# Turning the experts' inner units in row halves of the array

## The chip, the cores and the metric

The kernel runs on one core of one Trainium2 chip. The metric is the device time of one execution, in microseconds (us), of that core. A time is the median of several runs. The engines have short names: PE (TensorE, matmuls), PEld (its weight loads), DVE (VectorE), ACT (ScalarE), POOL (GpSimd), SP (the engine that issues most DMAs). PSUM, into which PE writes, is used here as eight banks of 128 partitions by 512 fp32 numbers.

## The reference

Two layers over x of shape (8, 512, 256), all fp32. The first adds to x a causal attention with 16 heads and a layer of 32 experts; the second adds a small two-layer network and a masked feed-forward layer. The change concerns the experts, which are, cut to what matters:

```python
probs = softmax(x @ gate_w.T + gate_b, axis=experts' tokens)
vals, idx = top_k(probs, 8)                 # eight tokens for each expert and batch
merged = sum over the eight of x[idx] * vals      # one row for each (batch, expert)
h = gelu(merged @ w1[e][:256] + w1[e][256])       # 256 -> 1024, last row is the first bias
o = h @ w2[e][:1024] + w2[e][1024]                # 1024 -> 256
out[b, idx] += o * vals
```

With 8 batches each expert has eight rows; the kernel pads them to 32 columns.

## The kernel before

Everything is laid out by a planner (class `Plan`). The code creates operations with `op(engine, cost, function, dependencies, priority, ...)`; `emit` then places them one by one on the engines, by the priorities and by the times that it reckons from the costs, and that fixes each engine's order of instructions. `acq` names what an operation takes: "b" is one PSUM bank, "w" is a pair of banks (there are four pairs), "eh" and "ehT" are single SBUF buffers. `rel` gives it back, at an entry such as `(tn, "w", 0, 2)` when the second of two readers is done.

Each PE operation has a mode. "R" stands for matmuls in row halves: two matmuls, one on partitions 0 to 63 and one on 64 to 127, each 64 rows deep, that write two different banks. "F" stands for the whole array, "E" and "C" for column slices. A change of mode adds `SWITCH` (96) to the cost in the planner, and a change to "F" a further `SECOND`; `choose` also prefers an operation in the mode of the one before it by `SAME`, half a unit of priority. These are the planner's numbers, not measured times.

The attention stage takes the largest part of the time. For each batch and each group of four heads (`produce`, 32 such groups) the queries, keys and values are projected, two tiles of 128 tokens at a time. `cross` (L337) runs a projection in two parts, all in row halves; between them the halves change places, and a VectorE memset of one small tile ("seen", L362) makes the second part wait until the first has been written. The projected tile tm is normalised and turned (L840, L330); `attend` computes scores, a softmax and the turned probabilities pr. `turn_halves` (L318) is the helper with which x, tm, gtm and pr are turned: for each block of 128 columns it issues two transposes, one for each half of the partitions, into the two banks of a pair.

The experts are spread through that stage, in eight groups of four (`expert`, L1177). A group runs like this:

- `hidden`: two halves of 512 inner units. Four experts at once write 32 partitions each of one bank (L1195); `h_out` copies the bank to `s.h`, the buffer eh (L1202).
- `turn`: four transposes of 128x128 for each half, in mode "F", into one bank (L1216). Partition and expert thereby become columns: the 128 columns of a block are four experts of 32.
- `bias`: one VectorE addition for each half, 512 numbers wide, of the turned first bias `eb1T` into the buffer ehT (L1227).
- `gelu`: ScalarE, in place, once both halves are added (L1222).
- `down`: the second weights, 32 columns at a time, out of ehT (L1255), and an addition into the output rows (L1262).

Weights are loaded by SP into a ring of five buffers. After the attention stage the outputs are joined (`combine`), and the second layer runs batch by batch.

Of the kernel before, what the change touches and what calls it, by code (L numbers as in the profile page):

```python
# [15 lines left out]
P = 128  # L16
# [3 lines left out]
H, D = 16, 64  # L20
# [9 lines left out]
EPG = 4  # L30
# [20 lines left out]
class Plan:  # L51
# [14 lines left out]
    def op(self, eng, cost, fn, deps, prio, acq=(), rel=(), mode="F", lat=0):  # L66
        o = Op()
        o.eng, o.cost, o.fn, o.prio, o.acq, o.rel, o.mode = eng, cost, fn, prio, acq, rel, mode
        o.deps = list(deps)
        o.end = lat  # L70
        self.ops.append(o)
        return o
# [148 lines left out]
def tile_two_layer_block(  # L221
# [26 lines left out]
    nc = tc.nc  # L248
# [12 lines left out]
    ident = const.tile([P, P], F32, tag="ident", name="ident")  # L261
# [27 lines left out]
    eb1T = const.tile([P, FH // P, E], F32, tag="eb1T", name="eb1T")  # L289
# [7 lines left out]
    with tc.tile_pool(name="pb", bufs=2) as pb, tc.tile_pool(name="pb1", bufs=1) as pb1:  # L297
# [8 lines left out]
        op = plan.op  # L306
# [3 lines left out]
        def w_tile(k=0):  # L310

            return plan.tile("w", k)

        def b_tile():

            return plan.tile("b")

        def turn_halves(dst, src, one=None, back=False):  # L318

            n = src.shape[1] // P
            for k in range(n):
                b = n - 1 - k if back else k
                for h in range(2):
                    rows = slice(h * D, (h + 1) * D)
                    out = dst[h][:, k * D : (k + 1) * D]
                    blk = src[rows, b * P : (b + 1) * P]
                    if one is None:
                        nc.tensor.transpose(out, blk, ident[rows, rows])  # L330
                    else:
                        nc.tensor.matmul(out, blk, one[rows, rows], start=True, stop=True)
# [81 lines left out]
        for q in range(NPR):  # L414
            consts.append(op("ACT", 675, lambda q=q: bias_rows(q), consts[1:2], -7.0 + 0.1 * q,
                             rel=["pr1"] if q == NPR - 1 else []))
# [72 lines left out]
        for k, f in enumerate(log1p_steps(lambda: oz, lambda: oy, lambda: oy2, lambda: om_sb)):  # L489
# [4 lines left out]
                   rel=["pr0"])]  # L494
# [155 lines left out]
        def turn_eb():  # L650
# [9 lines left out]
        v_eb = op("DVE", 334, lambda: nc.vector.tensor_copy(  # L660
            eb1T, early.pe[:, : FH // P * E].rearrange("p (k e) -> p k e", e=E)), [tb], 20.1,
            rel=[(tb, "b", 0)])
# [514 lines left out]
        def expert(g, when, ahead):  # L1177


            s = Grp()  # L1180
            s.pt = {}
            s.po = {}
            held = None
            out_ops = []
            for half in range(2):
                ld = load_stage(4 * g + half, when[half] - ahead)

                def hidden(half=half):
                    m = 4 * g + half
                    if half == 0:  # L1190
                        s.h = pb.tile([P, FH], F32, tag="eh", name=f"eh_{g}", bufs=1)
                    s.ph = b_tile()
                    for dc in range(NC):
                        for q in range(EPG):
                            nc.tensor.matmul(  # L1195
                                s.ph[32 * q : 32 * (q + 1), :], mT[:, dc, g * EPG + q, :],
                                ew[m, q][:, dc * 512 : (dc + 1) * 512],
                                start=(dc == 0), stop=(dc == NC - 1),
                            )

                def h_out(half=half):
                    nc.vector.tensor_copy(s.h[:, half * 512 : (half + 1) * 512], s.ph)  # L1202

                hd = op("PE", 1716, hidden, ld + merged, when[half], acq=["b"] + ["eh"] * (half == 0),
                        rel=["ew"] * EPG, mode="E")
                ho = op("DVE", 598, h_out, [hd], when[half] + 0.1, rel=[(hd, "b", 0)])

                def turn(half=half):
                    if half == 0:
                        s.hT = pb.tile(  # L1210
                            [P, FH // P, EPG, 32], F32, tag="ehT", name=f"ehT_{g}", bufs=1
                        )
                    s.pt[half] = b_tile()
                    for c in range(4):
                        k = half * 4 + c
                        nc.tensor.transpose(  # L1216
                            s.pt[half][:, c * P : (c + 1) * P], s.h[:, k * P : (k + 1) * P], ident
                        )

                def gelu(half=half):  # L1220
                    hT = s.hT[:, half * 4 : (half + 1) * 4]
                    nc.scalar.activation(hT, hT, AF.Gelu)  # L1222

                def bias(half=half):

                    c = slice(half * 4, (half + 1) * 4)
                    nc.vector.tensor_add(  # L1227
                        s.hT[:, c],
                        s.pt[half].rearrange("p (c q r) -> p c q r", c=4, q=EPG),
                        eb1T[:, c, g * EPG : (g + 1) * EPG].unsqueeze(3).to_broadcast(  # L1230
                            [P, 4, EPG, 32]
                        ),
                    )

                merged_used.append(hd)
                out_ops.append((ho, turn, bias, gelu))
            acts = []
            for half, (ho, turn, bias, gelu) in enumerate(out_ops):
                tn = op("PE", 436, turn, [out_ops[0][0], out_ops[1][0]], when[2] + 0.01 * half,
                        acq=["b"] + ["ehT"] * (half == 0), rel=["eh"] * (half == 1))  # L1240
                acts.append(op("DVE", 598, bias, [tn, v_eb], when[2] + 0.05 + 0.01 * half, rel=[(tn, "b", 0)]))
            gl = []
            for half, (ho, turn, bias, gelu) in enumerate(out_ops):
                gl.append(op("ACT", 586 + 1283 * (1 - half), gelu, acts, when[2] + 0.1 + 0.01 * half))
            prev = []
            for half in range(2):
                ld = load_stage(4 * g + 2 + half, when[3 + half] - ahead)

                def down(half=half):
                    m = 4 * g + 2 + half  # L1250
                    s.po[half] = b_tile()
                    for c in range(4):
                        for q in range(EPG):
                            k = half * 4 + c
                            nc.tensor.matmul(  # L1255
                                s.po[half][32 * q : 32 * (q + 1), :C], s.hT[:, k, q, :],
                                ew[m, q][:, c * C : (c + 1) * C],
                                start=(c == 0), stop=(c == 3),
                            )

                def o_out(half=half):
                    nc.vector.tensor_add(ebias[g], ebias[g], s.po[half][:, :C])  # L1262

                dn = op("PE", 1716, down, ld + gl, when[3 + half], acq=["b"],
                        rel=["ew"] * EPG + (["ehT", "eb"] if half else []), mode="E")
                prev = [op("DVE", 334, o_out, [dn] + prev,
                           when[3 + half] + 0.1, rel=[(dn, "b", 0)])]

            def o_send():
                for q in range(EPG):  # L1270
                    for hb in range(2):
                        nc.sync.dma_start(
                            o_all[g * EPG + q : P : E, hb, :],
                            ebias[g][32 * q + hb * BPG : 32 * q + (hb + 1) * BPG, :],
                        )

            experts_out.append(op("DMA", 500, o_send, prev, when[4] + 0.2, lat=2000))
# [14 lines left out]
        for g in range(NG):  # L1292
            h0, h1, d0, d1 = ((NHG + 2) * NU + step * (4 * g + k) + 0.7 for k in range(4))
            expert(g, [h0, h1, h1 + 3.0, d0, d1], step)
# [115 lines left out]
        for k in range(NFC // 2):  # L1410
# [9 lines left out]
            def out1(pt, k=k):  # L1420
# [6 lines left out]
                              merged_used, rel=["ew"] if k % 2 else []))  # L1427
# [389 lines left out]
```

## Time and profile before

| | |
|---|---|
| median of 3 runs | 1448.41 us (1447.43 to 1449.52) |
| the profiled execution | 1447.03 us, of which its span 1445.3 us |
| granted TensorE clock in it | 0.986 |
| first L1216 matmul, last | 287.6 us, 1016.5 us |
| first gelu of an expert group (L1222) | 294.4 us |
| first down product (L1255) | 315.9 us |

The span runs from the first to the last instruction; what lies around it is 1.7 us. Rows of the profile name the engine, the source line, the operation, and output<-inputs by the program's names. All PSUM banks are called w there, without a number. Many helpers have one line for all their uses: L330 is every transpose of `turn_halves`, L351 every matmul of `cross`, so the tile names tell them apart. A matmul's own duration overlaps those after it; what it costs PE is the distance between starts.

Busy shares in tenths over 40 equal slices of the span show the stages: start-up to the first slices, attention with the experts up to about slice 29, then the second layer.

```profile
PE   6789899999999999999999999999999799999999
DVE  4888877677767766776767677667766732332210
ACT  3577775576676666766766666656655532222221
POOL 4554555455555545555555555446544511011100
```

### The profile page before, as it was taken

What the parts mean: (1) busy time and instruction counts of PE and PEld (TensorE: products, weight loads), DVE (VectorE), ACT (ScalarE), POOL (GpSimd) and SP (SyncE); (2) the same over time, 40 slices, a digit from 0 to 9 for tenths busy, and PEclk for the clock granted to TensorE, in tenths of its full rate; (3) what the DMA queues carried; (4) which work ended last, traced back from release to release, by engine and by line L of the source; (5) the groups of instructions that cost most, each with busy time, mean ns of one, the idle gap of its engine ahead of it and who ended that gap; (6) DMA issues with size and microseconds to landing.
All of it is one profiled execution on the core that took longest, in us unless ns stands there. A gap on an engine that the chain in (4) does not pass through costs nothing.

```text
span 1445.3 us, 32547 instructions
## 1 busy us (share of the span) xinstructions
PE 1351.9 (94%) x11872; PEld 866.2 (60%) x11872; DVE 908.8 (63%) x3716; ACT 818.4 (57%) x2268; POOL 626.8 (43%) x1115
## 2 busy tenths in 40 slices
PE   6789899999999999999999999999999799999999
PEld 4455466557655665567557656565666466666665
DVE  4888877677767766776767677667766732332210
ACT  3577775576676666766766666656655532222221
POOL 4554555455555545555555555446544511011100
PEclk9899999999999999999999999999999899999999
DMA  6001000421143114113231241332120000000000
GB/s 210 5 2 45 30 2 1 162 85 68 61 131 123 59 60 137 60 60 122 74 122 60 64 143 49 103 109 88 62 73 16 1 15 1 16 15 19 19 16 21
DMA packets 74575, 90.65 MB, mean 63 GB/s; under 512 B 5272, under 2 KB 57744, under 8 KB 74416
## 3 DMA queue, kind: packets, MB, share of 16 engines
q1 hardware_dynamic: 73856, 88.16, 18.6%
q8 instruction: 93, 1.52, 0.4%
q14 instruction: 66, 0.54, 0.1%
q10 hardware_dynamic: 560, 0.43, 0.1%
HBM read 84.11 MB, written 4.19 MB: 61 GB/s over the span
## 4 chain that ended last, share of the span: by engine, by line
PE 68%; DVE 19%; ACT 7%; POOL 4%; issue 2%; DMA 1%; DVEq 0%; ACTq 0%; POOLq 0%
PE w L351 27%; PE w L1750 8%; PE w L1702 8%; PE w L1085 7%; PE w L1015 5%; PE w L330 5%; DVE pr L1024 4%; POOL rsqk L279 3%; DVE tm L840 2%; DVE ss L831 2%; DVE prT L1061 2%; PE w L1011 2%; ACT pr L1032 2%; ACT tm L812 1%; DVE kT L864 1%
## 5 line engine op out<-in xcount | busy, mean ns | idle before, releaser
L1042 POOL TENSOR_SCALAR pr<-pr,rinv 128x384 f32<-128x384 f32 (+3 forms) x512 | 295.3, 590 | 257.9 <-DVE rinv L1039 119.3
L1032 ACT ACTIVATE pr<-pr,nm 128x384 f32<-128x384 f32 (+3 forms) x512 | 286.5, 560 | 141.3 <-DVE nm L1024 110.2
L279 POOL TENSOR_TENSOR rsqk<-ss,nhalf 128x8 f32<-128x8 f32 x128 | 213.2, 1673 | 211.2 <-DVE ss L834 165.2
L351 PE MATMUL w<-wqk_sb,xnT 64*128 64x512 f32 x1024 | 269.8, 614 | 9.6 <-DVE seen L362 8.2
L1024 DVE CUSTOM_DVE_ANT_0 pr<-w,later 128x384 f32<-128x384 f32 (+3 forms) x512 | 240.3, 483 | 35.1 <-PE w L1015 33.9
L1015 PE MATMUL w<-kT,qT 64*128 64x384 f32 (+3 forms) x1024 | 198.5, 444 | 0.0
L351 PEld LDWEIGHTS w<-wqk_sb,xnT 64*128 64x128 f32 x1024 | 111.1, 190 | 86.8 <-issue 52.2
L1085 PE MATMUL w<-prT,v 128*64 128x512 f32 (+3 forms) x1024 | 156.8, 449 | 5.5 <-ACT prT L1059 4.2
L330 PEld LDWEIGHTS w<-ident,pr 64*128 64x128 f32 x2560 | 121.8, 139 | 61.3 <-issue 35.9
L330 PE MATMUL w<-ident,pr 64*128 64x64 f32 x2560 | 137.3, 227 | 8.8 <-DVE eh L1202 2.4
L1061 DVE COPY prT<-w 128x384 f32<-128x384 f32 (+3 forms) x256 | 122.7, 483 | 33.4 <-PE w L330 31.3
L351 PE MATMUL w<-wvg_sb,xnT 64*128 64x260 f32 x1024 | 141.9, 391 | 1.4 <-DVE seen L362 1.3
L1059 ACT COPY prT<-w 128x384 f32<-128x384 f32 (+3 forms) x256 | 105.7, 426 | 56.3 <-PE w L330 55.4
L1085 PEld LDWEIGHTS w<-prT,v 128*64 128x64 f32 x1024 | 70.6, 139 | 102.5 <-issue 66.3
L351 PE MATMUL w<-wp_sb,yT 64*128 64x256 f32 x1024 | 119.3, 379 | 1.8 <-DVE kT L864 0.8
L1702 PE MATMUL w<-xT,mT 128*128 128x512 f32 x256 | 120.9, 595 | 0.0
L831 DVE TENSOR_REDUCE ss<-sq 128x8 f32<-128x512 f32 x128 | 87.3, 682 | 52.1 <-ACT sq L816 51.6
L812 ACT COPY tm<-w 128x512 f32<-128x512 f32 x128 | 69.8, 586 | 86.2 <-PE w L351 84.0
L351 PEld LDWEIGHTS w<-wvg_sb,xnT 64*128 64x128 f32 x1024 | 101.1, 190 | 27.7 <-issue 8.7
L1015 PEld LDWEIGHTS w<-kT,qT 64*128 64x128 f32 x1024 | 95.0, 189 | 34.0 <-issue 28.2
L1011 PE MATMUL w<-gT,bst 64*128 64x384 bf16 (+3 forms) x512 | 94.2, 299 | 20.2 <-DVE nm L1024 8.6
L351 PEld LDWEIGHTS w<-wp_sb,yT 64*128 64x128 f32 x1024 | 102.2, 187 | 15.2 <-issue 3.4
(205 smaller groups left out, 1967.1 us busy)
## 6 DMA issues: line engine op xcount, KB each, us to landing
ew<-in_L_ffn_w_dram SPq DMA_DIRECT2D x128, 512.0 KB
x<-in_L_attn_x_dram SPq DMA_DIRECT2D x15, 512.0 KB
out_dram<-ot SPq DMA_DIRECT2D x32, 128.0 KB
raw<-in_L_ffn_w_dram SPq DMA_DIRECT2D x4, 512.0 KB
wqk_sb<-in_L_attn_Wk_dram SPq DMA_DIRECT2D x4, 256.0 KB
wqk_sb<-in_L_attn_Wq_dram SPq DMA_DIRECT2D x4, 256.0 KB
wp_sb<-in_L_attn_Wproj_dram SPq DMA_DIRECT2D x1, 1024.0 KB
b2g<-in_L_ffn_w_dram SPq DMA_DIRECT2D x32, 32.0 KB
```

The lines of the kernel that those rows point to most:

```text
L279: nc.gpsimd.tensor_tensor(r, src, nhalf[:, :n], ALU.pow)
L330: nc.tensor.transpose(out, blk, ident[rows, rows])
L351: x = nc.tensor.matmul(m.outs[i], lhs(i, k, rows), rhs(k, rows), start=(part == k == 0), stop=(part == 1 and k == n - 1))
L831: nc.vector.tensor_reduce(s.ss[t], s.sq[t], AX.X, ALU.add)
L1011: nc.tensor.matmul(m.sc[h][:, :w], bst[k, q, n0:w], s.gT[k, :w], start=True, stop=False)
L1015: nc.tensor.matmul(m.sc[h][:, :w], s.qT[k, q, n0:w], s.kT[k, q, :w], start=False, stop=True)
L1024: nc.vector.tensor_tensor_reduce(m.p[:, h, :], m.sc[h][:, :w], later[:, T - w :], -1.0, BIG, ALU.add, ALU.min, m.nm[:, h : h + 1],)
L1032: nc.scalar.activation(m.p[:, h, :], m.p[:, h, :], AF.Exp, bias=m.nm[:, h : h + 1], scale=-1.0, accum_out=m.sums[:, h : h + 1],)
L1042: nc.gpsimd.tensor_scalar(m.p[:, h, :], m.p[:, h, :], m.rinv[:, h : h + 1], 1.0, ALU.mult, ALU.mult)
L1061: nc.vector.tensor_copy(dst, src)
L1085: nc.tensor.matmul(pp.yp[h * D : (h + 1) * D, j * P :], s.v[j][:, hh * D : (hh + 1) * D], pp.tri[:, :, h, j : j + 4 * (NT - 1 - j) + 1 : 4 ...
L1702: nc.tensor.matmul(m.ph[i], w1T[:, dc, k * P : (k + 1) * P], s.xT[:, dc, :], start=(dc == 0), stop=False,)
```

## The change

The turn goes through `turn_halves`: for each half of the inner units four blocks of 128 columns, each as two transposes of 64 rows, so eight matmuls where there were four. Partitions 0 to 63 hold the first two experts of the group and 64 to 127 the other two, so bank 0 of the pair holds experts 0 and 1, and bank 1 experts 2 and 3, in the first 256 of the 512 columns. The operation takes a pair ("w") instead of a bank, and its mode is "R". The addition of the first bias is made bank by bank: two additions of 256 columns for each half, each an operation of its own with cost 334 instead of one of 598. The pair goes back after both. The gelu depends on all four additions of a group instead of two. Costs of the turns, priorities, the gelus and everything else stay as they are; the planner places all of it again.

```diff
-                    s.pt[half] = b_tile()
-                    for c in range(4):
-                        k = half * 4 + c
-                        nc.tensor.transpose(
-                            s.pt[half][:, c * P : (c + 1) * P], s.h[:, k * P : (k + 1) * P], ident
-                        )
+                    s.pt[half] = w_tile()
+                    turn_halves(s.pt[half], s.h[:, half * 4 * P : (half + 1) * 4 * P])
...
-                def bias(half=half):
+                def bias(bank, half=half):
 
                     c = slice(half * 4, (half + 1) * 4)
+                    q = slice(bank * 2, bank * 2 + 2)
+                    e = slice(g * EPG + bank * 2, g * EPG + bank * 2 + 2)
                     nc.vector.tensor_add(
-                        s.hT[:, c],
-                        s.pt[half].rearrange("p (c q r) -> p c q r", c=4, q=EPG),
-                        eb1T[:, c, g * EPG : (g + 1) * EPG].unsqueeze(3).to_broadcast(
-                            [P, 4, EPG, 32]
-                        ),
+                        s.hT[:, c, q],
+                        s.pt[half][bank][:, : 4 * D].rearrange("p (c q r) -> p c q r", c=4, q=2),
+                        eb1T[:, c, e].unsqueeze(3).to_broadcast([P, 4, 2, 32]),
                     )
...
                 tn = op("PE", 436, turn, [out_ops[0][0], out_ops[1][0]], when[2] + 0.01 * half,
-                        acq=["b"] + ["ehT"] * (half == 0), rel=["eh"] * (half == 1))
-                acts.append(op("DVE", 598, bias, [tn, v_eb], when[2] + 0.05 + 0.01 * half, rel=[(tn, "b", 0)]))
+                        acq=["w"] + ["ehT"] * (half == 0), rel=["eh"] * (half == 1), mode="R")
+                acts += [op("DVE", 334, lambda k=k, f=bias: f(k), [tn, v_eb],
+                            when[2] + 0.05 + 0.01 * half, rel=[(tn, "w", 0, 2)]) for k in range(2)]
```

The helper that the turn now calls, unchanged:

```python
for k in range(n):
    b = n - 1 - k if back else k
    for h in range(2):
        rows = slice(h * D, (h + 1) * D)
        out = dst[h][:, k * D : (k + 1) * D]
        blk = src[rows, b * P : (b + 1) * P]
        if one is None:
            nc.tensor.transpose(out, blk, ident[rows, rows])
```

## The prediction

> **What bounds the kernel now.** I read the page first, then the windows by stage, then the timeline around the eight places where the touched line runs. The page's head, its first part and its chain of waits:
>
> ```profile
> span 1445.3 us, 32547 instructions
> PE 1351.9 (94%) x11872; PEld 866.2 (60%) x11872; DVE 908.8 (63%) x3716; ACT 818.4 (57%) x2268; POOL 626.8 (43%) x1115
> PE 68%; DVE 19%; ACT 7%; POOL 4%; issue 2%; DMA 1%; DVEq 0%; ACTq 0%; POOLq 0%
> ```
>
> TensorE (PE) is the bound: busy for 94% of the span and 68% of the chain that ends last; VectorE (DVE) has 19%. The experts run inside the attention stage, so I asked for that stretch alone (columns: stretch, busy microseconds and instruction counts of PE, PEld, DVE, ACT, POOL, then granted clock, DMA share and GB/s):
>
> ```profile
> 290.00:1065.00 775.00, 740.19 (x7470) 475.57 (x7468) 555.80 (x2266) 508.43 (x1473) 408.10 (x709) 1.00 0.26 85
> ```
>
> There PE leaves 775.0 − 740.2 = 34.8 us idle, DVE works 555.8 / 775 = 72% of it, and the granted clock is 1.00. So PE time taken out of this stage counts, except where PE stands waiting anyway.
>
> **The turns as they are.** L1216 appears eight times, once per expert group. In four groups (near 407, 508, 818 and 919 us) both halves run together, always between the two parts of a value projection. PE's timeline there:
>
> ```profile
> 507.23 0.59 PE L330 MATMUL w<-ident,pr 64*128 64x64 f32 x12
> 507.66 1.09 PE L351 MATMUL w<-wvg_sb,xnT 64*128 64x260 f32 x8
> 508.68 1.09 PE L1216 MATMUL w<-ident,eh 128*128 128x128 f32 x8
> 509.70 1.15 PE L351 MATMUL w<-wvg_sb,xnT 64*128 64x260 f32 x8
> 510.69 0.66 PE L330 MATMUL w<-ident,tm 64*128 64x64 f32 x16
> ```
>
> The first column is the start; differences of starts are what an item costs PE. Read three things:
> - Twelve half transposes (64 rows, 64 columns) take 507.66 − 507.23 = 0.43 us, 36 ns each.
> - Eight full transposes take 509.70 − 508.68 = 1.02 us. Their eight weight loads spread over 0.86 us with 0.14 for the last, so one step is (0.86 − 0.14)/7 = 0.10 to 0.11 us: 0.87 for the eight, and 0.15 left for going back to half rows.
> - The eight projection matmuls before them take 1.02 us. A run of 32 such matmuls, all in half rows, starts at 528.35 with its successor at 531.86: 3.51/32 = 0.11 each, 0.88 for eight. The other 0.14 to 0.15 is the step from half rows to full.
>
> So a joint visit costs 0.15 + 1.02 = 1.17 us of PE.
>
> **The change, part by part.**
>
> *Turns in row halves.* Eight full transposes become sixteen half ones per group: 16 × 0.036 = 0.57 us, with no change of row mode on either side. A joint visit falls from 1.17 to 0.57: **−0.60**, half of it from the two mode changes, half from the faster steps.
>
> Is that time on the path? The second part of the projection waits for a VectorE memset, "seen", that follows the first part:
>
> ```profile
> 508.95 0.06 DVE L362 MEMSET seen<- 1x2 f32 x1
> 509.38 0.69 DVE L1227 TENSOR_TENSOR ehT<-w,eb1T 128x512 f32<-128x512 f32 x1 [0.28 <-PE w L1216]
> 509.98 0.72 DVE L840 TENSOR_TENSOR tm<-tm,rsqk 128x512 f32<-128x512 f32 x1
> ```
>
> The memset ends at 509.01 and PE goes on only at 509.70, so the full transposes hold it. With half ones the first part ends at 507.66 + 0.88 = 508.54, the turns at 509.11, still behind the memset: the second part comes 0.59 earlier. What is late next is the turn of tm at 510.69, whose second tile is scaled until 509.98 + 0.72 = 510.70; PE must find 0.6 us of other work (there are score tiles and probability turns that need only VectorE and GpSimd results). I count it in full, since the stage leaves PE so little idle: 4 × 0.59 = **−2.4**.
>
> In the other four groups (near 288, 601, 704 and 1012) the halves run apart, two visits of four. PE's timeline and the memset at one of them:
>
> ```profile
> 601.09 0.65 PE L1216 MATMUL w<-ident,eh 128*128 128x128 f32 x4
> 602.05 0.06 DVE L362 MEMSET seen<- 1x2 f32 x1
> 602.19 1.99 PE L351 MATMUL w<-wqk_sb,xnT 64*128 64x512 f32 x8 [0.45 <-DVE seen L362]
> 604.86 0.66 PE L1216 MATMUL w<-ident,eh 128*128 128x128 f32 x4
> 605.97 0.29 PE L332 MATMUL w<-ident,gtm 64*128 64x64 bf16 x8 [0.46 <-POOL gtm L943]
> ```
>
> Here PE waits behind both visits, 0.45 us for the memset and 0.46 for GpSimd's gtm. Two visits hold four mode changes (0.6) and the same 0.3 of faster steps: 0.9 per group. If all waits only grow, the gain is nothing; if the list places the turns elsewhere, it is 0.9. No row shows the new order. Of the chain before, PE is 68%; but at these places a wait follows, so I take half: 4 × 0.45 = **−1.8**.
>
> A rule that speaks against the first part: the Trainium skill, "TensorEngine Tiling (Array Packing)", section "Instruction Overhead", says that a matmul carries some 60 cycles whatever its width and that no tiling factor should be taken from a small dimension. Here the moving width is 64, and the count doubles. By that rule 16 × 64 columns cost as much as 8 × 128, and only the mode changes are won: 4 × 0.30 + 4 × 0.60 / 2 = 2.4 instead of 4.2 us. The row of 36 ns against 109 measures this very form with its weight loads, so I take the row.
>
> *First bias bank by bank.* Two adds of 512 elements per group become four of 256. Rows by shape:
>
> ```profile
> L1120 DVE TENSOR_TENSOR x<-w,x 128x256 f32<-128x256 f32 x32 | 12.7, 419 | 15.6 <-PE w L351 15.6
> L1227 DVE TENSOR_TENSOR ehT<-w,eb1T 128x512 f32<-128x512 f32 x16 | 10.9, 682 | 1.1 <-PE w L1216 1.1
> ```
>
> That is 2 × 0.419 − 0.682 = 0.156 us more per half, 16 × 0.156 = 2.5 us of VectorE over the run. L1120 also reads PSUM and SBUF at 256 wide; the interleaved output is not in the trace. Hidden under PE it costs 0, wholly on the path 2.5. VectorE has 19% of the chain: **+0.5**. Queued behind the adds on VectorE are the scaling of tm, the memsets and the row maxima, for which PE and ScalarE wait.
>
> *Gelu after four adds instead of two, second weights.* The first gelu is at 294.4 us and the first down product reads its result at 315.9; 0.3 us more is covered by 20. Without that cover it would be 8 × 0.3 = 2.5 us. No DMA is added; SP's and GpSimd's queues get nothing new of their own.
>
> *Whole pairs of banks.* Each turn now takes a pair of banks instead of one bank, two of the four pairs for two turns where one pair's halves served. A turn that finds no pair is put off by the planner; only a pair that comes free later than planned makes PE stand, with every later matmul queued behind. Bounds: 0, or the 1.1 us of the longest PE wait behind a turn (1016.15 to 1017.91) in each group, 8.8. A pair now goes back after two adds of 0.42 rather than a bank after one of 0.68, about the same time, so I take 0 and keep 8.8 for the range.
>
> *A new order.* From the first turn at 287 us on, the planner places everything anew, because the turn's mode no longer costs a change and is preferred half a unit earlier. Four groups repeat the same pattern to 0.01 us (1.02, 1.02, 0.98), so a disturbance dies out within a group instead of running on. I allow ±2 us.
>
> **Sum.** −2.4 − 1.8 + 0.5 = −3.7. Against the profiled execution, 1447.03 us with its span of 1445.3, that is 1443.3. It ran 1.4 below the median of 1448.41, so the comparable figure is **1444.7**.
>
> **Rivals.**
> 1. *The turn is only a filler* (no measurable change). The full turns stand in gaps of a projection; shorten them and PE waits for the memset, the tm scale or gtm. For: the waits after 602 and 605, the scale ending at 510.70. Against: 0.69 us between memset and PE in the joint groups, and 34.8 us idle in 775. Gain 4 × 0.3 of mode changes, less 0.5: 1447.7.
> 2. *The gaps close completely.* All 6.0 us of PE come out (4 × 0.60 + 4 × 0.90) and the earlier due turns let a little more close up, up to 2 us: 1441.
> 3. *Bank pairs run out* (slower). At 508.5 a projection and a probability turn (copied until 509.01) hold a pair each; two turns would hold the other two until four adds, 1.7 us of VectorE, are through, and the tm turns need two more. For: the skill's same page, "Gotcha 1: PSUM Pressure", warns that row tiles write different banks; which bank is held when, this trace does not show. Against: the planner counts pairs. At 1.1 per group: 8.8 − 3.7 = +5.1, 1453.5. It makes the kernel slower once the wait passes 3.7/8 = 0.46 us per group.
> 4. *The change doesn't do what it says*: if the halves did not overlap, 16 × 0.11 = 1.75 per group against 1.17, +4.6 in all. The same helper overlaps for pr and tm, so I give it nothing of its own.
>
> **Chances.** Forecast 0.45, filler 0.2, closing up 0.1, pairs or an unlucky order 0.25. The range runs from the second rival less the unknown order (1439.5) to the third (1453). About 0.2%, 2.9 us, is what a measurement of this kernel can tell from no change. Faster by more (below 1445.5): most of the forecast's case and all of the closing up, 0.48. Slower by more (above 1451.3): 0.27. Within: 0.25.
>
> **What would show it.** The changed profile should have no L1216; in its place 128 matmuls of 64x64 out of eh at L330, some 36 ns apart, with the projections on both sides at 0.88 instead of 1.02. The adds should read 128x256, x32, at about 420 ns. PE busy in the stage should fall by some 6 us. A wait of PE on the ehT adds would speak for the pairs; longer waits on the memset or tm for the filler. The forecast is wrong if PE's busy time falls and its idle time rises by as much.

## The result, and the profile after

The changed kernel takes 1453.01 us (median of 7 runs, 1452.58 to 1454.71), the kernel before beside it 1447.94. The ratio is 1.0036 (95% interval 1.0027 to 1.0045): 5.1 us slower, where 3.7 us less had been forecast.

The page of the changed kernel, its head, first part and chain of waits:

```profile
span 1450.9 us, 32720 instructions
PE 1355.1 (93%) x11936; PEld 865.7 (60%) x11936; DVE 910.1 (63%) x3732; ACT 824.2 (57%) x2270; POOL 633.7 (44%) x1115
PE 66%; DVE 18%; ACT 8%; POOL 4%; issue 2%; DMA 0%; DVEq 0%; ACTq 0%; POOLq 0%
```

TensorE is still the bound, and its share fell from 94% to 93% while the span grew. Two counts are worth a look. ScalarE has two instructions more (2270 against 2268), though no activation was added. And TensorE's busy time rose (1355.1 us against 1351.9), though the turns were to make it fall.

To see where, I set the two traces beside each other at equal amounts of matmul work done (each matmul counted by its columns and its share of the array, the turns of eh left out). The attention stage from 280 to 1065 us of the kernel before holds the same work as 280.0 to 1071.3 us of the changed kernel (columns as in the prediction; first before, then after):

```profile
280.00:1065.00 785.00, 748.81 (x7560) 480.24 (x7558) 564.88 (x2298) 516.37 (x1497) 414.52 (x715) 1.00 0.27 87
```

```profile
280.00:1071.30 791.30, 751.52 (x7610) 478.15 (x7608) 566.90 (x2315) 522.24 (x1497) 417.95 (x713) 0.99 0.27 89
```

For the same work TensorE is busy 2.7 us longer and idle 3.6 us longer (39.8 against 36.2). The busy time is longer because more of it ran at half the granted clock. The trace before has one such stretch of 3.4 us in this part (at 457.9 us), the changed kernel six (at 289.5, 463.5, 603.5, 709.3, 876.5 and 1016.5 us), here the first:

```profile
289.50:292.90 3.40, 3.19 (x16) 1.44 (x18) 3.27 (x18) 1.98 (x9) 2.52 (x5) 0.51 0.81 259
```

The 16 values products that fall mostly into it take 3.54 us from start to next start, against 2.31 before. An estimate from these figures: if half of each stretch is lost, 748.8 − 1.7 = 747.1 us of full-clock work before stand against 751.5 − 10.2 = 741.3 after. So matmul time of about 5.8 us did leave, the 6 us that the prediction named as its sign; the slower stretches put back some 8.5 us of busy time, and the waits 3.6. The same sum gives 747.1 to 747.5 us for the three experiments below with full turns in nearly the old order (the new order by itself, the pair alone, the gelu alone), and 741.4 to 742.6 for three with turns in halves in the changed order (the changed kernel's repetition, the first group put back, the gelus in one piece).

Where does the delay arise? At equal work the changed kernel is 0.0 us late at 280 us, 4.7 at 320, 6.0 at 380, and then stays near that but for passing excursions to 9 (at 600 and 1020): 5.7 at 660, 6.8 at 780, 5.9 at 1060, 5.5 at the end. The net loss arises around the first expert group; behind it, gains and losses balance.

TensorE's timeline there, first of the kernel before, then of the changed one:

```profile
287.58 0.66 PE L1216 MATMUL w<-ident,eh 128*128 128x128 f32 x4
288.41 0.66 PE L1216 MATMUL w<-ident,eh 128*128 128x128 f32 x4 [0.17 <-DVE nm L1024]
```

```profile
287.56 0.27 PE L330 MATMUL w<-ident,eh 64*128 64x64 f32 x1
288.43 0.46 PE L330 MATMUL w<-ident,eh 64*128 64x64 f32 x7 [0.60 <-DVE nm L1024]
...
302.35 0.41 PE L330 MATMUL w<-ident,eh 64*128 64x64 f32 x8
...
310.32 1.98 PE L351 MATMUL w<-wqk_sb,xnT 64*128 64x512 f32 x6 [1.04 <-DVE nm L1024]
...
314.49 0.59 PE L330 MATMUL w<-ident,pr 64*128 64x64 f32 x11 [1.66 <-ACT qT L858]
```

The first turn starts where it started, at 287.6. The second, at 288.4 before, now comes at 302.4. And near 310 to 315 TensorE waits for a row maximum and for qT, a ScalarE output. ScalarE's timeline in that stretch says why:

```profile
304.54 1.28 ACT L1218 ACT_TABLE_LOAD   x1
305.84 0.63 ACT L1218 ACTIVATE ehT<-ehT 128x512 f32<-128x512 f32 x1
306.49 1.28 ACT L1032 ACT_TABLE_LOAD   x1
...
309.87 1.28 ACT L1218 ACT_TABLE_LOAD   x1
311.17 0.63 ACT L1218 ACTIVATE ehT<-ehT 128x512 f32<-128x512 f32 x1
...
312.07 1.28 ACT L1032 ACT_TABLE_LOAD   x1
```

The gelus wait for all four additions, so they come eleven microseconds later than before, when the softmax already has exponentials to run. They fall between these and are torn apart: gelu table, gelu, exp table, exponentials, gelu table, gelu, exp table. That is four table loads of 1.28 us in 9 us instead of two, and these are the two extra instructions of the page. In the kernel before the same two gelus stood behind one load, and the exp table was loaded only at 304.5 us, when ScalarE had waited 2.12 us for a row maximum anyway:

```profile
293.13 1.28 ACT L1222 ACT_TABLE_LOAD   x1
294.42 0.63 ACT L1222 ACTIVATE ehT<-ehT 128x512 f32<-128x512 f32 x1
...
295.95 0.65 ACT L1222 ACTIVATE ehT<-ehT 128x512 f32<-128x512 f32 x1
...
304.48 1.28 ACT L1032 ACT_TABLE_LOAD   x1 [2.12 <-DVE nm L1024]
```

### The profile page after: what moved, and what is told of

Same layout as the page of the kernel before. It is cut to its first block, busy times and chain, and to the rows that moved or that the text cites. A ratio compares the mean times of both kernels' runs of the same rounds, so it can differ in the third digit from the quotient of the medians.

```text
span 1450.9 us, 32720 instructions
## 1 busy us (share of the span) xinstructions
PE 1355.1 (93%) x11936; PEld 865.7 (60%) x11936; DVE 910.1 (63%) x3732; ACT 824.2 (57%) x2270; POOL 633.7 (44%) x1115
## 4 chain that ended last, share of the span: by engine, by line
PE 66%; DVE 18%; ACT 8%; POOL 4%; issue 2%; DMA 0%; DVEq 0%; ACTq 0%; POOLq 0%
PE w L351 25%; PE w L1085 8%; PE w L1747 8%; PE w L1699 8%; PE w L330 5%; PE w L1015 5%; DVE pr L1024 4%; DVE tm L840 3%; POOL rsqk L279 3%; ACT pr L1032 2%; DVE ss L831 2%; ACT tm L812 2%; PE w L1011 2%; DVE prT L1061 1%; DVE kT L864 1%
## 5 line engine op out<-in xcount | busy, mean ns | idle before, releaser
L1042 POOL TENSOR_SCALAR pr<-pr,rinv 128x384 f32<-128x384 f32 (+3 forms) x512 | 303.6, 606 | 260.9 <-DVE rinv L1039 136.3
L1085 PE MATMUL w<-prT,v 128*64 128x512 f32 (+3 forms) x1024 | 166.2, 470 | 6.0 <-ACT prT L1059 3.1
L330 PE MATMUL w<-ident,pr 64*128 64x64 f32 x2560 | 133.7, 227 | 13.9 <-POOL pr L1042 4.0
L1085 PEld LDWEIGHTS w<-prT,v 128*64 128x64 f32 x1024 | 73.8, 145 | 99.0 <-issue 71.6
L858 ACT ACTIVATE qT<-w,w 128x128 f32<-128x128 f32 x256 | 90.8, 366 | 40.2 <-PE w L330 20.6
```

What stands on the lines that cost most here:

```text
L1042: nc.gpsimd.tensor_scalar(m.p[:, h, :], m.p[:, h, :], m.rinv[:, h : h + 1], 1.0, ALU.mult, ALU.mult)
L1085: nc.tensor.matmul(pp.yp[h * D : (h + 1) * D, j * P :], s.v[j][:, hh * D : (hh + 1) * D], pp.tri[:, :, h, j : j + 4 * (NT - 1 - j) + 1 : 4 ...
```

## The experiments

The theory after this reading: the half transposes save time; the second pair of banks makes the first group's second turn late; the late turn makes the gelus late and torn. Rivals: the half transposes themselves cost the time; any new order of the plan does; the preference for mode R does.

**The form of the turn, in the changed kernel's order.** The plan is kept to the last operation; only the body of the turn goes back to four full transposes.

```diff
-                    turn_halves(s.pt[half], s.h[:, half * 4 * P : (half + 1) * 4 * P])
+                    for c in range(4):
+                        k = half * 4 + c
+                        nc.tensor.transpose(
+                            s.pt[half][0][:, c * P : (c + 1) * P], s.h[:, k * P : (k + 1) * P], ident)
```

> The changed kernel with its operations planned exactly as they are there (a pair of banks, mode R, four additions of 256), but each turn made of four full transposes into one bank, so only the form of the turn differs. Theory A (the new order of the operations costs the time, the half transposes themselves save some): slower than the changed kernel by 8 x 0.3 to 0.6 us, 1455 to 1458 us. Theory B (the half transposes themselves cost it, because their thin matmuls let the TensorE clock drop): at least 3 us faster than the changed kernel, 1450 or less, with fewer half-clock stretches.

Measured: 1455.85 us, 1.0055 of before (1.0043 to 1.0068), against 1.0036 for the changed kernel. The two intervals meet only at their edges: the half transposes save about 0.19% or 2.8 us, and the order around them costs more than the whole loss. Its runs were granted 0.977 to 0.979 of the clock, the changed kernel's 0.973 to 0.979, so it is not the thin transposes that lower the clock. The price of one turn can be read where it stands between the same neighbours, first in the changed kernel, then in this one:

```profile
410.49 0.46 PE L330 MATMUL w<-ident,eh 64*128 64x64 f32 x8
410.79 1.10 PE L351 MATMUL w<-wvg_sb,xnT 64*128 64x260 f32 x8
```

```profile
412.12 0.66 PE L1216 MATMUL w<-ident,eh 128*128 128x128 f32 x4
412.70 1.15 PE L351 MATMUL w<-wvg_sb,xnT 64*128 64x260 f32 x8
```

From start to start 0.30 us against 0.58. The rival of the costly halves falls.

**The halves, in the old order.** The plan of the kernel before is made with its own costs and then carried out in that order, but seven of the eight groups turn in halves into two banks. The first group stays whole: in the old order all four pairs are taken there, and by the plan the values product that follows the turns would have no bank.

```diff
+        WHOLE = (0,)
...
-                    s.pt[half] = b_tile()
+                    if g in WHOLE:
+                        s.pt[half] = b_tile()
...
+                    else:
+                        s.pt[half] = [plan.tile("b", k) for k in range(2)]
+                        turn_halves(s.pt[half], s.h[:, half * 4 * P : (half + 1) * 4 * P])
```

> The kernel before with its own plan replayed in the same order, but seven of the eight expert groups turn in row halves, each half into two banks, and add their first bias in four additions of 256. The first group stays whole, since in the old order all four pairs of banks are taken there. Theory A (order): the direct gain appears, 7 x 0.3 to 0.6 us less 2 us of extra VectorE time at most: 1444 to 1447 us, not slower than before. Theory B (halves and clock): 1450 us or more, with more half-clock stretches than before.

Measured: 1447.91 us, ratio 0.9999 (0.9991 to 1.0007): not slower, but no gain that can be told either. At equal work its trace gains 1.9 us on the kernel before between 280 and 1020 us. The gain can be placed. Near 509 us both halves run together; TensorE's rows there, of this experiment (with its own line numbers) and, last, of the kernel before:

```profile
508.23 1.10 PE L371 MATMUL w<-wvg_sb,xnT 64*128 64x260 f32 x8
...
514.47 1.99 PE L371 MATMUL w<-wqk_sb,xnT 64*128 64x512 f32 x8 [0.17 <-DVE seen L382]
```

```profile
514.49 1.99 PE L351 MATMUL w<-wqk_sb,xnT 64*128 64x512 f32 x8 [0.17 <-DVE seen L362]
```

From the first projection part (507.66 in the kernel before, shown in the prediction) this takes 6.24 us instead of 6.83: 0.59 less. The four groups with joint turns (407, 508, 818 and 919 us) gain 0.6 each, 2.5 us together. The groups near 705 and 1012, with turns apart, gain nothing, and the one near 601 stands beside a half-clock stretch that hides what it does. Such a stretch costs about 0.6 us here once the waits behind it have taken up the rest: the kernel before has one at 457.9 that this one lacks, this one has one at 869.3 that the kernel before lacks, and the distance of the traces moves by 0.6 us at each. At the start of the second layer, where nothing was edited, over 2 us are given back, behind another one at 1118.5 that is 6.8 us long. So the direct gain is there, in the joint groups alone, and the whole time does not show it.

**The gelus in one piece.** In the changed kernel, one ScalarE operation for both:

```diff
-            gl = []
-            for half, (ho, turn, bias, gelu) in enumerate(out_ops):
-                gl.append(op("ACT", 586 + 1283 * (1 - half), gelu, acts, when[2] + 0.1 + 0.01 * half))
+            gl = [op("ACT", 2 * 586 + 1283, lambda: [f() for _, _, _, f in out_ops], acts, when[2] + 0.1)]
```

> The changed kernel with the two gelus of an expert group planned as one ScalarE operation (cost 2 x 586 + 1283), both activations one behind the other. In the changed kernel's trace the first group's gelus stand apart, at 305.8 and 311.2 us, with four activation-table loads of 1.28 us instead of two, and TensorE idles 3.3 us near 308 to 315. Theory A1 (that split is the main loss): two table loads fewer and 3 to 4 us faster, 1449 to 1450 us. Rival (the loss is spread, or in the bank pairs): under 1.5 us faster.

Measured: 1450.95 us, ratio 1.0024 (1.0015 to 1.0034). Both extra loads are gone, and 2.1 us with them (1453.01 to 1450.95, the kernel before at 1447.94 and 1447.83), though the two intervals overlap. That is less than expected. The traces say more: at equal work this one loses 1.9 us between 280 and 380 us where the changed kernel loses 6.0, and it has no half-clock stretch there. So the torn gelus, with the stall and the slower stretch that go with them, are a good part of the loss, not all of it.

**One pair for both halves.** Each half fills only 256 of a bank's 512 columns, so both fit into one pair; the first bias then takes two additions of 512.

```diff
+                    s.pt = w_tile()
+                    turn_halves(s.pt, s.h)
...
+            tn = op("PE", 872, turn, [out_ops[0][0], out_ops[1][0]], when[2],
+                    acq=["w", "ehT"], rel=["eh"], mode="R")
+            acts = [op("DVE", 598, lambda k=k: bias(k), [tn, v_eb], when[2] + 0.05 + 0.01 * k,
+                       rel=[(tn, "w", 0, 2)]) for k in range(2)]
```

> Both halves of a group are turned in one operation (cost 872, mode R) into one pair of banks, 512 columns each, and the first bias is added by two additions of 512, one for each bank. Theory A2 (the second pair of banks, for which the first group's second turn waits from 287.6 to 302.4 us, starts the loss): the group's turns come together, the first gelus come near 294 us again, and it is faster than before: 1443 to 1447 us. Rival (any new order costs as much): 1451 or more.

Measured: median 1453.26 us, ratio 1.0041 (1.0027 to 1.0054), though the profiled run took 1447.65 and the four others 1453.1 to 1454.3. In the profiled run the first group's loss is gone (first gelu at 294.8), but the third and the seventh group now have their gelus 8 us apart, with two more table loads each. At equal work the trace loses 3.2 us at the third (496 to 552 us) and 3.6 at the seventh (904 to 952). The expectation failed. Why the unprofiled runs lie 5 us above the profiled one, no trace shows.

**The first group put back.** The changed kernel, with group 0 turned as before and the other seven as changed:

```diff
+            if g == 0:
...
+                    tn = op("PE", 436, turn, [out_ops[0][0], out_ops[1][0]], when[2] + 0.01 * half,
+                            acq=["b"] + ["ehT"] * (half == 0), rel=["eh"] * (half == 1))
+                    acts.append(op("DVE", 598, bias, [tn, v_eb], when[2] + 0.05 + 0.01 * half, rel=[(tn, "b", 0)]))
+            else:
...
```

> The changed kernel, but the first expert group is turned as in the kernel before (full transposes, one bank for each half, two additions of 512); the other seven groups as changed. Theory A2 (the whole loss arises in the first group, whose second turn finds no free pair of banks and comes 14.8 us later): the 5 to 6 us of the changed kernel are gone, 1446 to 1448.5 us. Rival (every new order costs, the first group only happens to be the first): 1451 us or more.

Measured: 1447.95 us where the kernel before took 1449.61 on that chip: ratio 0.9986 (0.9977 to 0.9995). Slower by 0.36% becomes faster by 0.14%. The first group alone makes 0.50% or 7 us, and the other seven bring about 2 us (0.7 to 3.3). Where these arise its own trace does not show: at equal work with the trace before it is 0.9 us late at 380 us and 1.2 at 1060, with four half-clock stretches in between (458.7, 598.6, 704.4, 1011.6). These stretches alone, then, do not make a kernel slower than before. The first group's gelus stand behind one load again (ScalarE's timeline):

```profile
293.89 1.28 ACT L1218 ACT_TABLE_LOAD   x1
295.19 0.63 ACT L1218 ACTIVATE ehT<-ehT 128x512 f32<-128x512 f32 x1
296.71 0.65 ACT L1218 ACTIVATE ehT<-ehT 128x512 f32<-128x512 f32 x1
```

**One pair and one gelu operation.** The single pair (fourth experiment) and the single gelu operation (third) in one kernel.

> Both halves turned in one operation into one pair of banks, two additions of 512, and both gelus in one ScalarE operation. With one pair alone the third and the seventh group still have their gelus 8 us apart with two more table loads each. If split gelus are what remains there, 1444 to 1447 us and no more than 16 activation-table loads before 1100 us; if the median of the one-pair kernel (1453.3) comes from something else, 1450 or more again.

Measured: 1444.47 us, ratio 0.9962 (0.9949 to 0.9974): faster than both kernels. Its first group (ScalarE's timeline), with the two activations now merged into one row:

```profile
294.29 1.28 ACT L1218 ACT_TABLE_LOAD   x1
295.59 1.15 ACT L1218 ACTIVATE ehT<-ehT 128x512 f32<-128x512 f32 x2
```

Each of the eight groups has exactly one gelu load and one exp load. At the third and the seventh group, where the single pair alone lost 3.2 and 3.6 us, this trace loses 0.5 and 0.9.

**A new order by itself.** The kernel before with one planner's cost changed, no other edit:

```diff
-                tn = op("PE", 436, turn, [out_ops[0][0], out_ops[1][0]], when[2] + 0.01 * half,
+                tn = op("PE", 416, turn, [out_ops[0][0], out_ops[1][0]], when[2] + 0.01 * half,
```

> The kernel before with one planner's number changed (the turn's cost 416 instead of 436) and no other edit, so the planner may place operations anew though the work is the same. It measures what a new order alone does. If orders are worth several us each, it differs from before by 2 us or more; if the plan is robust, within 1 us.

Measured: ratio 1.0008 (0.9999 to 1.0018), 1.2 us at the middle, not clear of nothing. The order does change, but little: all turns keep their pattern, joint or apart.

**The mode alone.** Full transposes in one bank, planned as mode R:

```diff
-                        acq=["b"] + ["ehT"] * (half == 0), rel=["eh"] * (half == 1))
+                        acq=["b"] + ["ehT"] * (half == 0), rel=["eh"] * (half == 1), mode="R")
```

> The kernel before with the full transposes planned as mode R (no change of mode in the plan), everything else as before: one bank, two additions of 512. It separates the planner's preference from the pair of banks. Theory A2 (the pair): the first group's turns stay together and it is within 2 us of before. Rival (the preference for the mode moves the turns and costs the time): 1451 us or more.

Measured: ratio 1.0000 (0.9990 to 1.0009), and the first group's turns stay together at 286.6 us. The preference moves turns in later groups and costs nothing.

**The pair alone.** Full transposes, mode F, two additions; each turn takes a pair and uses one bank of it:

```diff
-                    s.pt[half] = b_tile()
+                    s.pt[half] = w_tile()[0]
...
-                        acq=["b"] + ["ehT"] * (half == 0), rel=["eh"] * (half == 1))
+                        acq=["w"] + ["ehT"] * (half == 0), rel=["eh"] * (half == 1))
...
```

> The kernel before with full transposes, mode F and two additions of 512, but each turn takes a whole pair of banks and uses one of the two. Theory A2 (the pair of banks makes the first group's second turn wait): the first group's turns come apart by some 15 us again and the time is 1450 to 1455 us on the scale where before is 1448. Rival (it takes the halves or the four additions to lose time): within 1 us of before.

Measured: 1450.96 us, ratio 1.0020 (1.0011 to 1.0029). TensorE's timeline:

```profile
287.63 0.66 PE L1216 MATMUL w<-ident,eh 128*128 128x128 f32 x4
...
301.54 0.66 PE L1216 MATMUL w<-ident,eh 128*128 128x128 f32 x4
...
312.05 2.90 PE L351 MATMUL w<-wqk_sb,xnT 64*128 64x512 f32 x7 [2.27 <-DVE kT L864]
```

The same picture without any of the rest: the second turn 13 us late, gelus at 303.2 and 308.9 with four table loads, and a wait of TensorE of 2.3 us. At equal work the trace is 0.1 us late at 280, 2.6 at 310, before any half-clock stretch, and 4.0 at 320, behind one at 313.3. In the other seven groups the turns keep the pattern of before, joint or apart. The pair by itself makes the kernel slower, and putting the first group back makes the changed one faster than before: together they show the cause of the sign.

**The gelu operation alone**, in the kernel before (the edit of the third experiment):

> The kernel before with the two gelus of a group in one ScalarE operation and no other edit. It tells how much of the gain of the kernel with one pair and one gelu operation (ratio 0.9962) is the gelu's. If the gelu alone makes it: 0.9962 to 0.998. If it is the half transposes and the single pair: 0.999 to 1.001.

Measured: ratio 1.0005 (0.9996 to 1.0014). It gains nothing there, since no gelus of that kernel are torn apart. The gain of the best version is of both edits together.

**The changed kernel once more**, on the chip of the last two:

> The changed kernel once more, on the chip of this call, so that the ratios of the two others can be set beside it. All theories: 1.003 to 1.0045 of before.

Measured: 1453.96 us, ratio 1.0037 (1.0024 to 1.0049). Its gelus are torn in the same place, at 305.7 and 311.1.

## Why the prediction was wrong

*Whole pairs of banks, the step that failed.* It was priced at 0, with 8.8 us as the other end, on this ground: a turn that finds no pair is put off by the planner, and only a pair that comes free later than planned makes TensorE stand. The first half of the sentence happened, and was itself the price. Being put off was counted as free. In the first group the second turn was put off by 14 us, with it two additions and both gelus, and these met the exponentials. By the plan the same shortage arises in the four groups that were joint before, where the halves come apart too, but there a pair is back after 3.0 us (turns at 407.5 and 410.5) and the gelus stay together. The pair alone makes the kernel 0.20% slower; putting the first group back moves the changed one by 0.50%. How the 0.50% splits is not settled: to the torn gelus go 2.1 us by the medians of the third experiment and about 4 by its trace at equal work, slower clock included; the rest goes to the late turn in this order and what follows it.

*The gelu.* "0.3 us more is covered by 20" looked only at who reads the gelu's result, the down products. The question not asked was what stands around it on its own engine. The rule was at hand: the Trainium skill, "ScalarE: Activation LUTs", section "Table sets: the hidden batching unit", says to batch activations by table set, because each change of set is a load. The row agrees and gives the size: 1.28 us per load, two more loads, and four of them within 9 us on the path of qT and the row maxima.

*The clock.* The prediction read 1.00 for the stage and gave the clock no term. In the changed kernel half-clock stretches put back some 8.5 us of TensorE's busy time in the stage (the estimate above). What five stretches more cost in the end is not settled; at the 0.6 us each that the second experiment's trace shows it would be about 3 us, an estimate.

*The turns in halves.* The mechanism was right: 0.30 against 0.58 us for one turn in one place, as worked out from 36 ns and 109. The term was too large: 4.2 us of gain against about 2.8 by the first experiment and 2 for seven groups, additions included, by the fifth. The second experiment shows which half of it: in the old order the four joint groups gain 2.5 us where 2.4 were forecast, and two of the groups with turns apart gain nothing where 0.45 each were forecast. There the filler rival was right. The rule that the prediction held against this part, by which only the mode changes would be won, is not borne out: eight half transposes in 0.30 us are 37 ns each, less than half the 109 of a full one.

*The additions.* Forecast 2.5 us more of VectorE in all; the row reads

```profile
L1225 DVE TENSOR_TENSOR ehT<-w,eb1T 128x256 f32<-128x256 f32 x32 | 12.8, 413 | 0.0
```

against 10.9 before, so 1.9 us. Right, and small.

*A new order, ±2 us.* In keeping with two controls (1.0008, at most 1.0018, and 1.0000), and so is the argument that a disturbance dies out within a group: behind 380 us the lag stays near 6 us. What the argument missed is that in one group no pair came back for 14 us. (The lower end of the range, 1439.5, is 0.5 us above the prediction's own sum, 1441 less 2; nothing rests on it.)

*The rival of the bank pairs* named the resource and came out at 1453.5 us. That it is so close to the measured time is luck: it spread 1.1 us of waiting over eight groups, where one group lost it all.

## What to carry to other kernels

When a step takes more of a scarce buffer, look for the tightest place of the schedule, not the average one: the price is not the wait for the buffer but everything that slides with the step that was put off. Follow the sliding step to each engine that it feeds and ask what is next to it there; on ScalarE a late activation of another table set costs two loads and not only its delay. And before a second buffer is taken, see whether the first is full: here both halves fit into one pair, and with the two gelus bound together that version is the fastest of all (0.9962).

## What the runs showed of the hardware

**Half the clock behind idle time.** TensorE's granted clock falls to half for 3.4 us at a time. Between 200 and 1065 us the starts of these stretches lie, in each trace, whole multiples of 3.41 us apart (in the changed kernel 51, 92, 123, 172 and 213 behind the first), so the time can be cut into windows of that length. In the thirteen traces a stretch followed each of the 20 windows in which TensorE idled more than 1.75 us by the profile, none of the 1839 in which it idled less than 1.0, and 15 of the 140 between. So a stall can cost more than its length, and it matters where it falls. The changed kernel and its repetition have the same stall near 309 to 316 us. In the repetition one window holds 2.18 us of the idle time, and half clock follows (the clock is the third number from the end):

```profile
308.90:312.30 3.40, 2.25 (x7) 0.68 (x6) 1.15 (x5) 3.35 (x8) 1.83 (x4) 1.00 0.00 0
312.30:315.70 3.40, 1.22 (x14) 0.89 (x16) 0.58 (x6) 3.39 (x10) 0.30 (x1) 1.00 0.02 5
315.70:319.10 3.40, 3.40 (x16) 1.54 (x14) 0.71 (x4) 1.12 (x4) 1.06 (x2) 0.51 0.00 0
```

In the first trace the stall is shared by two windows, 1.19 and 1.44 us, and the clock stays:

```profile
309.97:313.39 3.42, 2.23 (x7) 0.81 (x7) 0.72 (x4) 3.38 (x5) 1.71 (x4) 1.00 0.00 0
313.39:316.80 3.41, 1.97 (x17) 1.14 (x19) 1.12 (x6) 3.17 (x10) 1.30 (x2) 1.00 0.02 5
316.80:320.20 3.40, 3.40 (x55) 2.13 (x55) 2.39 (x9) 2.77 (x8) 0.06 (x1) 1.00 0.00 0
```

Such stretches are more frequent in the changed kernel (mean granted clock 0.973 to 0.979 over its first seven runs) than in the kernel before (0.981 to 0.986 in the runs of the first experiments). That they cause a part of the loss is argued, not shown; no experiment kept the clock up and the order as it was.
